# Making the first pair's gates of layer 1's second mixture in parts during the causal attention

## The chip, the cores and the metric

The kernel runs on one core of one Trainium2 chip. A core has five engines with a queue each: PE (matrix products, whose results go into one of the kernel's eight "bank" tiles of 128 x 512), DVE (vector work), ACT (functions of one operand), POOL (general work) and SP, which here only issues transfers. Between engines, semaphores carry the dependences. The metric is device time in microseconds (us), smaller is better. Before the change it is 1533.77 us, the median of 3 runs (1532.04 to 1535.4).

## The reference

A stack of four layers on x of 4 images (b) x 512 tokens x 128 features, fp32. Each layer is half a mixture of experts, an attention (or a scan), and half a mixture again. Cut to what the change touches, layer 1's attention and the mixture that follows it:

```python
x = x + _L1_attn_ref(_layernorm(x), Wq1, Wk1, Wq2, Wk2, Wv, Wo, bo)
#   logits = A1 * A2 * SCALE per head (16 heads), causal, softmax, times v, times Wo
x = x + 0.5 * _L1_ffn_ref(_layernorm(x), gate_weight, w_gate, w_up, w_down, ws_gate, ws_up, ws_down)

def _L1_ffn_ref(...):
    scores = jax.nn.sigmoid(x @ gate_weight.T)            # 8 experts
    topk_w, topk_idx = jax.lax.top_k(scores, 2)
    topk_w = 2.5 * topk_w / (topk_w.sum(-1, keepdims=True) + 1e-20)
    combine = einsum('tk,tke->te', topk_w, one_hot(topk_idx))
    y_e = (silu(x @ w_gate[e].T) * (x @ w_up[e].T)) @ w_down[e].T
    return einsum('te,teh->th', combine, y) + shared      # shared: one more expert, no gate
```

After it come layer 2's mixture, scan and mixture, and then layer 3's first mixture.

## The kernel before, in words

x stays in SBUF as one tile for each image, xs[b], 128 tokens by 4 by 128. Layer 1 uses all experts on all tokens: two experts of 64 rows fill the 128 partitions, so there are 4 chunks and a fifth for the shared expert.

The attention (`attention`, called by `l1_attn`) goes through 16 units, an image and four of its 16 heads each, and each unit through 4 key blocks j. Its order on PE, DVE, ACT and POOL is written out by hand: the scores of the next unit (L610, then the largest on DVE, L627 and L631, and the exponentials on ACT, L644, or a subtraction on POOL, L642), the transposed weights of this one (L655, L664, L666), and their products with the values (L677, into acc, copied by ACT at L761). Between them, small generators get a turn: `begin_next` the next image's norm and factors, and `go_on` whatever `after(b)` returned when image b was through (`ended`, L789 and L1236). In layer 1 `after` is None. Each key block offers up to two such turns. Rows q_a and k_a are fetched by SP for units ahead (L1206) and multiplied at L1213.

The mixture (`l1_ffn`) works on a pair of images. `normed_T` makes the norm of both (statistics L160 and L161 on DVE; variance to the power -1/2 and offsets on POOL, L164 to L169; application by turns on DVE, L178, and ACT, L174), transposes them on PE (L187) and copies them to nT (L1049). `scored` makes the scores (L1058), a sigmoid follows (L1083), then the choice of two experts, some 17 small instructions on DVE (L218 to L231 twice, L1108 to L1115), giving comb. `to_rows` transposes comb (L1071), copies it (L1073) and stores it to DRAM as rows, expert by token (L1075); the transfer at L1124 reads the rows back, each spread over 64 partitions, as cb, 2 transfers of 512 KB for each image. For each chunk `up` makes two products (L1092, L1093), a sigmoid (L1096) and two multiplications on DVE (L1097, L1098); POOL multiplies the gated chunks by cb (L1147); `down` is the second product (L1135), and L1153 adds it to xs[b].

The stage after the attention ("chain") is a generator `behind` for each pair: this mixture, layer 2's mixture, scan and mixture, and the tokens of layer 3's mixture. `skewed(gens, lag)` gives each live generator one step a round, the second from round `lag` on. POOL's order there is the order of this program; PE, DVE, ACT and SP are ordered by the planner, from its own estimates. It may also place work of this stage earlier, where its inputs are there and its memory is not taken from the stage's own pool; norms and nT come from a pool that lives through the whole kernel (`work`).

The tiles of the stage's own pool (decay, gates, cb, h and others) take memory that the attention used.

Of the kernel before, what the change touches and what calls it, by code (L numbers as in the profile page):

```python
# [9 lines left out]
FP = mybir.dt.float32  # L10
# [31 lines left out]
def kernel(ctx: ExitStack, tc: tile.TileContext, a: dict, out: bass.AP):  # L42
# [95 lines left out]
    def load_T(ap, rows, cols, name, tag=None):  # L138

        dst = pools["w"].tile([cols, rows], FP, name=name, tag=tag or name)  # L140
        m = min(rows, P)
        k = rows // m
        raw = stage.tile([m, k, cols], FP, name=f"raw_{name}", tag="raw")
        nc.sync.dma_start(raw, ap.rearrange("(k m) c -> m k c", m=m))
        ps = bank(f"ps_{name}")
        for i in range(k):
            nc.tensor.transpose(ps[:cols, i * m : (i + 1) * m], raw[:, i, :], ident[:m, :m])
        copy(dst, ps[:cols, :rows])
        return dst


# [914 lines left out]

    def to_rows(pool, gates, i, tag):

        pc = bank(f"gT_{tag}")
        for t in range(NT):  # L1070
            nc.tensor.transpose(pc[:E, t * P : (t + 1) * P], gates[:, i * NT + t, :], ident)  # L1071
        gT = pool.tile([E, S], FP, name=f"gT_{tag}", tag="gT")
        nc.scalar.copy(gT, pc[:E, :])  # L1073
# [3 lines left out]

    def l1_ffn(pool, i, bs):
        tag = f"f1{i}_{bs[0]}"
        G = len(bs) * NT  # L1080
        nTs = yield from normed_T(pool, bs, tag)
        sc = pool.tile([P, G, E], FP, name=f"sc_{tag}", tag="sc1")
        nc.scalar.activation(sc, scored(nTs, l1["gate"], tag), AF.Sigmoid)  # L1083
        order = [NC] + list(range(NC))
# [16 lines left out]

        up(0, 0)
        yield
        m1, s1 = route(pool, sc, G, "0")
        rest = without(pool, sc, m1, G, -4.0, "0")
        m2, s2 = route(pool, rest, G, "1")
        total = pool.tile([P, G], FP, name=f"total_{tag}", tag="total")
        nc.vector.tensor_tensor(total, s1, s2, ALU.add)  # L1108
        nc.vector.tensor_scalar(total, total, 1e-20, None, ALU.add)
        nc.vector.reciprocal(total, total)  # L1110

        comb = pool.tile([P, G, E], FP, name=f"comb_{tag}", tag="comb")
        nc.vector.tensor_tensor(comb, m1, m2, ALU.add)
        nc.vector.scalar_tensor_tensor(comb, comb, 2.5, sc, ALU.mult, ALU.mult)
        nc.vector.tensor_tensor(comb, comb, bc(total, [P, G, E]), ALU.mult)  # L1115
        up(0, 1)
        yield
        cbs = []
        for x, b in enumerate(bs):
            rows = to_rows(pool, comb, x, f"{b}_{tag}")  # L1120

            cb = pool.tile([P, NC, S], FP, name=f"cb{b}_{tag}", tag="spread", bufs=4)
            for u in range(2):
                nc.sync.dma_start(  # L1124
                    cb[u * I1 : (u + 1) * I1],
                    bass.AP(tensor=rows.tensor, offset=rows.offset + u * S, ap=[[0, I1], [2 * S, NC], [1, S]]),
                )
# [90 lines left out]

    def l1_attn(beside, begun):
        begin_, fetch_, project_, future, early = begun  # L1220
        with tc.tile_pool(name="attn1", bufs=2) as pool:
# [13 lines left out]
            def residual(b, po):  # L1235
                nc.vector.tensor_tensor(xs[b], po, xs[b], ALU.add)  # L1236

            attention(pool, "a1_", begin, project, residual, l1["wo"], lambda h: future, None,
                beside(pool), fetch,
# [224 lines left out]
    def whole(parts):  # L1464
        for _ in parts:
            pass
# [57 lines left out]
    with tc.tile_pool(name="weights12", bufs=1) as mid:  # L1524
# [12 lines left out]
        with tc.tile_pool(name="ahead1", bufs=2) as ahead:  # L1537
# [15 lines left out]

            l1_attn(lambda pool: prep_l3_ffn(xs[0]), begun)

        def behind(pool, bs):
            yield from l1_ffn(pool, 1, bs)
            yield from l2_ffn(pool, 0, bs)
# [10 lines left out]
        with tc.tile_pool(name="chain", bufs=2) as pool:  # L1569
# [13 lines left out]
            with tc.manual_schedule(engines={mybir.EngineType.Pool}):  # L1583
                whole(skewed([behind(pool, bs) for bs in pairs], 8))
        pools["w"] = wpool
# [54 lines left out]
```

## Time and profile before

| what | us |
|---|---|
| median of 3 runs | 1533.77 |
| the profiled execution | 1513.06 |
| its span, first to last instruction | 1511.3 |
| attention of layer 1, from the first scores to proj_a | 515.76 to 740.15 |
| chain stage, from there to the last indirect transfer's issue | 740.15 to 1012.1 |
| PE busy, of the span | 1271.2 (84%) |
| DVE, ACT, POOL busy | 880.3, 682.8, 694.0 |

The profile is of one execution. A group line of it reads: line of the kernel, engine, operation, written tile <- read tiles, shapes, count, then busy time; a timeline line gives start and length, and in brackets how long the engine stood idle before it and what ended that. PE's clock is given as a share of full speed. Where a line belongs to a helper (norms, transposes), the tile's name tells which call it is: names ending in _f are of a mixture, in _a of an attention.

### The profile page before, as it was taken

What the parts mean: (1) busy time and instruction counts of PE and PEld (TensorE: products, weight loads), DVE (VectorE), ACT (ScalarE), POOL (GpSimd) and SP (SyncE); (2) the same over time, 40 slices, a digit from 0 to 9 for tenths busy, and PEclk for the clock granted to TensorE, in tenths of its full rate; (3) what the DMA queues carried; (4) which work ended last, traced back from release to release, by engine and by line L of the source; (5) the groups of instructions that cost most, each with busy time, mean ns of one, the idle gap of its engine ahead of it and who ended that gap; (6) DMA issues with size and microseconds to landing.
All of it is one profiled execution on the core that took longest, in us unless ns stands there. A gap on an engine that the chain in (4) does not pass through costs nothing.

```text
span 1511.3 us, 28774 instructions
## 1 busy us (share of the span) xinstructions
PE 1271.2 (84%) x10645; PEld 816.7 (54%) x10645; DVE 880.3 (58%) x2890; ACT 682.8 (45%) x1431; POOL 694.0 (46%) x808
## 2 busy tenths in 40 slices
PE   4787999995969999999878878729689999998394
PEld 3465666774746666667555656616433333333173
DVE  5236767763355657767456566525367787774343
ACT  1235877871422367767522222103236655564042
POOL 5346767871433678868323111464431223312343
PEclk9897999995999999999999888759879999999597
DMA  9410240002513884231022000023105000000223
GB/s 262 101 53 22 79 170 12 9 7 73 151 37 65 223 258 145 87 121 44 4 64 49 1 1 1 28 71 91 60 15 177 15 7 10 14 3 15 78 78 112
DMA packets 100660, 106.21 MB, mean 70 GB/s; under 512 B 9084, under 2 KB 73832, under 8 KB 100520
## 3 DMA queue, kind: packets, MB, share of 16 engines
q1 hardware_dynamic: 91752, 90.11, 20.7%
q0 software_dynamic: 6656, 13.22, 2.5%
q8 instruction: 84, 1.38, 0.4%
q10 hardware_dynamic: 2112, 1.05, 0.3%
q14 instruction: 56, 0.46, 0.1%
HBM read 62.49 MB, written 41.85 MB: 69 GB/s over the span
## 4 chain that ended last, share of the span: by engine, by line
PE 70%; DVE 9%; POOL 8%; DMA 5%; issue 5%; ACT 3%; SPq 1%; POOLq 0%; ACTq 0%; DVEq 0%
PE s_a L610 13%; PE t_a L655 10%; PE o_f L515 6%; PE h_f L479 6%; PE acc_a L677 5%; PE acc_a L749 5%; PE y_f L1329 3%; PE t_a L610 3%; POOL disp_f L408 2%; PE ot_a L768 2%; PE gu_f L1092 2%; PE lg_f L322 1%; POOL rstd_f L165 1%; DVE low L699 1%; PE gu_f L1093 1%
## 5 line engine op out<-in xcount | busy, mean ns | idle before, releaser
L642 POOL TENSOR_SCALAR sc_a<-sc_a,top_a 128x128 f32<-128x128 f32 (+3 forms) x256 | 274.8, 1089 | 84.7 <-DVE top_a L627 55.8
L610 PE MATMUL s_a<-k_a,q_a 32*128 32x512 f32 (+3 forms) x1536 | 263.4, 544 | 7.0 <-DVE top_a L631 3.7
L719 ACT ACTIVATE w_a<-t_a 128x512 f32<-128x512 f32 x256 | 140.4, 595 | 116.6 <-PE t_a L610 86.9
L699 DVE TENSOR_REDUCE low<-s_a 128x1 f32<-128x512 f32 x256 | 163.4, 684 | 45.4 <-PE t_a L610 32.7
L655 PE MATMUL t_a<-ident,sc_a 128*128 128x128 f32 x1280 | 174.3, 283 | 4.3 <-DVE top_a L631 3.8
L610 PE MATMUL t_a<-ql_a,k_a 32*128 32x512 f32 x512 | 167.2, 644 | 0.3 <-DVE low L699 0.2
L501 POOL DMA_INDIRECT res_f<-y_f,back_f x112 | 109.8, 980 | 124.6 <-ACT y_f L500 90.3
L655 PEld LDWEIGHTS t_a<-ident,sc_a 128*128 128x128 f32 x1280 | 144.6, 144 | 41.0 <-issue 16.5
L644 ACT ACTIVATE sc_a<-sc_a,top_a 128x128 f32<-128x128 f32 (+3 forms) x256 | 135.0, 575 | 12.8 <-DVE top_a L631 12.2
L610 PEld LDWEIGHTS s_a<-k_a,q_a 32*128 32x128 f32 x1536 | 91.5, 187 | 79.1 <-issue 41.9
L664 ACT ACTIVATE w_a<-t_a 128x256 f32<-128x256 f32 (+2 forms) x192 | 94.2, 526 | 71.0 <-PE t_a L655 70.8
L408 POOL DMA_INDIRECT disp_f<-n_f,to_f x96 | 94.8, 988 | 56.2 <-issue 35.8
L515 PE MATMUL o_f<-w_l,h_f 128*128 128x128 f32 (+1 forms) x896 | 109.6, 277 | 0.0
L515 PEld LDWEIGHTS o_f<-w_l,h_f 128*128 128x128 f32 (+1 forms) x896 | 102.1, 184 | 8.0 <-DVE back_f L464 4.4
L479 PE MATMUL h_f<-dT_f,w_l 128*128 128x320 f32 (+1 forms) x256 | 104.1, 544 | 2.8 <-ACT dT_f L457 2.8
L677 PE MATMUL acc_a<-w_a,vpad 128*32 128x128 f32 x2560 | 98.2, 280 | 0.0
L666 ACT COPY w_a<-t_a 128x256 f32<-128x256 f32 (+2 forms) x192 | 93.5, 527 | 5.0 <-PE t_a L655 4.7
L631 DVE CUSTOM_DVE_ANT_0 sc_a<-s_a,future 128x128 f32<-128x128 f32 (+3 forms) x128 | 62.3, 487 | 47.7 <-PE s_a L610 39.0
L1147 POOL TENSOR_TENSOR h_f<-h_f,cb_f 128x512 f32<-128x512 f32 x32 | 40.7, 1286 | 104.4 <-DVE h_f L1098 62.7
L631 DVE CUSTOM_DVE_ANT_0 sc_a<-s_a,table 128x128 f32<-128x128 f32 (+3 forms) x128 | 62.3, 487 | 43.5 <-PE s_a L610 38.3
L500 ACT ACTIVATE y_f<-o_f,d_f 128x128 f32<-128x128 f32 (+1 forms) x112 | 39.0, 394 | 98.0 <-DVE o_f L495 94.1
L749 PE MATMUL acc_a<-w_a,vpad 128*32 128x256 f32 x1024 | 82.1, 391 | 1.0 <-DVE low L699 0.9
(341 smaller groups left out, 2182.8 us busy)
## 6 DMA issues: line engine op xcount, KB each, us to landing
fac_a<-fac_a_sb SPq DMA_DIRECT2D x36, 256.0 KB, 4.9
disp_f<-zeros_f SPq DMA_DIRECT2D x4, 2080.0 KB, 10.6
d_f<-disp_f SPq DMA_DIRECT2D x32, 260.0 KB, 3.0
w_l<-in_L_ffn_w_dram SPq DMA_DIRECT2D x16, 512.0 KB, 7.2
cb_f<-rows_f SPq DMA_DIRECT2D x16, 512.0 KB, 8.4
q_a<-fac_a SPq DMA_DIRECT2D x32, 256.0 KB, 3.5
k_a<-fac_a SPq DMA_DIRECT2D x32, 256.0 KB, 3.8
r_f<-res_f SPq DMA_DIRECT2D x16, 256.0 KB, 2.8
```

The lines of the kernel that those rows point to most:

```text
L408: nc.gpsimd.indirect_dma_start(out=self.to[c][i0 + t][:, :], out_offset=bass.IndirectOffsetOnAxis(ap=to[:, c, t : t + 1], axis=0), in_=ns[ ...
L479: nc.tensor.matmul(ps[u][:, :cap], w1[:, e, (c + u) * P : (c + u + 1) * P], dT, start=True, stop=True)
L515: nc.tensor.matmul(po[:m, s, :], h[:, c, s * P : s * P + m], w2[:, e, c, :], start=(c == 0), stop=(c == NC - 1),)
L610: nc.tensor.matmul(ps[:, n0:n1], q[r : r + SLOT, i * P : (i + 1) * P], k[r : r + SLOT, n0:n1], start=True, stop=True)
L631: nc.vector.tensor_tensor_reduce(sc, banks[r][:, :n], more, -1.0, HUGE, ALU.add, ALU.min, top)
L642: nc.gpsimd.tensor_scalar(sc, sc, top, None, ALU.subtract)
L644: nc.scalar.activation(sc, sc, AF.Exp, bias=top, scale=-1.0)
L655: nc.tensor.transpose(ps[:, x * n + j * P : x * n + (j + 1) * P], st["sc", u, i, r0 + x][:, j * P : (j + 1) * P], ident,)
L677: nc.tensor.matmul(st["acc", u][r * SLOT : (r + 1) * SLOT, i * P : (i + 1) * P], vpads[b % 2][:, j, g * 4 + r, :], st["w", u, i, r][:, j * ...
L699: nc.vector.tensor_reduce(st["low", u][:, i, c : c + 1], ps, AX.X, ALU.max, negate=True)
L719: nc.scalar.activation(w, ps, AF.Exp)
L749: nc.tensor.matmul(acc[r * SLOT : (r + 1) * SLOT, n0:n1], vpads[b % 2][:, j, g * 4 + r, :], st["w", u, j, r][:, n0:n1], start=(j == 0 and ...
```

## The change

Five edits. `l1_ffn` for the first pair no longer makes its norm, transposes, scores, choice and rows; a new generator `l1_early` makes them in 20 parts, handed to the attention as `after(1)`, so that its turns run from the end of image 1 on (`after` of the other images is empty). Its norm is the fine form: two tiles of statistics or of application a part. Since ACT computes exponentials in the attention, the sigmoid is made there as 1 / (1 + exp(-s)), by an exponential on ACT and an addition and a reciprocal on DVE. The choice is taken out into `chosen`, which the second pair uses as before, all at once. Small tiles of `l1_early` come from a new pool ("gates10") opened around the attention, its rows' copies from `work`. The lag of the chain stage goes from 8 rounds to 4. `norms`, `route`, `without`, `transposed` and `scored` are called as they are.

```diff
@@ -147,6 +147,14 @@
             nc.tensor.transpose(ps[:cols, i * m : (i + 1) * m], raw[:, i, :], ident[:m, :m])
         copy(dst, ps[:cols, :rows])
         return dst
+
+    def made_of(parts):
+
+        while True:
+            try:
+                next(parts)
+            except StopIteration as end:
+                return end.value
 
 
     def norms(srcs, dsts, tag, on="vector", fine=False):
@@ -1064,23 +1072,74 @@
             )
         return plg[:, : len(nTs) * NT * E].rearrange("p (g e) -> p g e", e=E)
 
-    def to_rows(pool, gates, i, tag):
+    def chosen(pool, sc, G, tag):
+
+        m1, s1 = route(pool, sc, G, "0")
+        yield
+        rest = without(pool, sc, m1, G, -4.0, "0")
+        m2, s2 = route(pool, rest, G, "1")
+        yield
+        total = pool.tile([P, G], FP, name=f"total_{tag}", tag="total")
+        nc.vector.tensor_tensor(total, s1, s2, ALU.add)
+        nc.vector.tensor_scalar(total, total, 1e-20, None, ALU.add)
+        nc.vector.reciprocal(total, total)
+        comb = pool.tile([P, G, E], FP, name=f"comb_{tag}", tag="comb")
+        nc.vector.tensor_tensor(comb, m1, m2, ALU.add)
+        nc.vector.scalar_tensor_tensor(comb, comb, 2.5, sc, ALU.mult, ALU.mult)
+        nc.vector.tensor_tensor(comb, comb, bc(total, [P, G, E]), ALU.mult)
+        return comb
+
+    def l1_early(pool, bs, got):
+
+
+        tag = f"f11_{bs[0]}"
+        G = len(bs) * NT
+        ns = [work.tile([P, NT, D], FP, name=f"n{b}_{tag}", tag="n", bufs=3) for b in bs]
+        yield from norms([xs[b] for b in bs], ns, tag, "both", True)
+        nTs = []
+        for n, b in zip(ns, bs):
+            yield
+            nT = work.tile([P, S], FP, name=f"nT{b}_{tag}", tag="nT", bufs=4)
+            copy(nT, transposed(n, f"{b}_{tag}"))
+            nTs.append(nT)
+            yield
+        sc = pool.tile([P, G, E], FP, name=f"sc_{tag}", tag="sc1")
+        for x in range(len(bs)):
+            yield
+
+            nc.scalar.activation(
+                sc[:, x * NT : (x + 1) * NT], scored(nTs[x : x + 1], l1["gate"], f"{x}_{tag}"), AF.Exp, scale=-1.0
+            )
+        yield
+        nc.vector.tensor_scalar(sc, sc, 1.0, None, ALU.add)
+        nc.vector.reciprocal(sc, sc)
+        comb = yield from chosen(pool, sc, G, tag)
+        rows = []
+        for x, b in enumerate(bs):
+            yield
+            rows.append(to_rows(work, comb, x, f"{b}_{tag}", "n", 3))
+        got[:] = nTs, rows
+
+    def to_rows(pool, gates, i, tag, of="gT", bufs=2):
 
         pc = bank(f"gT_{tag}")
         for t in range(NT):
             nc.tensor.transpose(pc[:E, t * P : (t + 1) * P], gates[:, i * NT + t, :], ident)
-        gT = pool.tile([E, S], FP, name=f"gT_{tag}", tag="gT")
+        gT = pool.tile([E, S], FP, name=f"gT_{tag}", tag=of, bufs=bufs)
         nc.scalar.copy(gT, pc[:E, :])
         rows = dram.tile([E, S], FP, name=f"rows_{tag}", tag=f"rows_{tag}")
         nc.sync.dma_start(rows, gT)
         return rows
 
-    def l1_ffn(pool, i, bs):
+    def l1_ffn(pool, i, bs, early=None):
         tag = f"f1{i}_{bs[0]}"
         G = len(bs) * NT
-        nTs = yield from normed_T(pool, bs, tag)
-        sc = pool.tile([P, G, E], FP, name=f"sc_{tag}", tag="sc1")
-        nc.scalar.activation(sc, scored(nTs, l1["gate"], tag), AF.Sigmoid)
+        if early:
+            nTs, rows = early
+        else:
+            nTs = yield from normed_T(pool, bs, tag)
+            sc = pool.tile([P, G, E], FP, name=f"sc_{tag}", tag="sc1")
+            nc.scalar.activation(sc, scored(nTs, l1["gate"], tag), AF.Sigmoid)
         order = [NC] + list(range(NC))
         hs = {}
 
@@ -1099,31 +1158,23 @@
             hs[x, k] = h
 
 
-        up(0, 0)
-        yield
-        m1, s1 = route(pool, sc, G, "0")
-        rest = without(pool, sc, m1, G, -4.0, "0")
-        m2, s2 = route(pool, rest, G, "1")
-        total = pool.tile([P, G], FP, name=f"total_{tag}", tag="total")
-        nc.vector.tensor_tensor(total, s1, s2, ALU.add)
-        nc.vector.tensor_scalar(total, total, 1e-20, None, ALU.add)
-        nc.vector.reciprocal(total, total)
-
-        comb = pool.tile([P, G, E], FP, name=f"comb_{tag}", tag="comb")
-        nc.vector.tensor_tensor(comb, m1, m2, ALU.add)
-        nc.vector.scalar_tensor_tensor(comb, comb, 2.5, sc, ALU.mult, ALU.mult)
-        nc.vector.tensor_tensor(comb, comb, bc(total, [P, G, E]), ALU.mult)
-        up(0, 1)
-        yield
+        if not early:
+            up(0, 0)
+            yield
+            comb = made_of(chosen(pool, sc, G, tag))
+            up(0, 1)
+            yield
+            rows = []
         cbs = []
         for x, b in enumerate(bs):
-            rows = to_rows(pool, comb, x, f"{b}_{tag}")
+            if not early:
+                rows.append(to_rows(pool, comb, x, f"{b}_{tag}"))
 
             cb = pool.tile([P, NC, S], FP, name=f"cb{b}_{tag}", tag="spread", bufs=4)
             for u in range(2):
                 nc.sync.dma_start(
                     cb[u * I1 : (u + 1) * I1],
-                    bass.AP(tensor=rows.tensor, offset=rows.offset + u * S, ap=[[0, I1], [2 * S, NC], [1, S]]),
+                    bass.AP(tensor=rows[x].tensor, offset=rows[x].offset + u * S, ap=[[0, I1], [2 * S, NC], [1, S]]),
                 )
             cbs.append(cb)
         for x, b in enumerate(bs):
@@ -1216,7 +1267,7 @@
 
         return begin, fetch, project, future, {}
 
-    def l1_attn(beside, begun):
+    def l1_attn(beside, begun, after):
         begin_, fetch_, project_, future, early = begun
         with tc.tile_pool(name="attn1", bufs=2) as pool:
             def begin(b):
@@ -1235,7 +1286,7 @@
             def residual(b, po):
                 nc.vector.tensor_tensor(xs[b], po, xs[b], ALU.add)
 
-            attention(pool, "a1_", begin, project, residual, l1["wo"], lambda h: future, None,
+            attention(pool, "a1_", begin, project, residual, l1["wo"], lambda h: future, after,
                 beside(pool), fetch,
             )
 
@@ -1551,10 +1602,15 @@
             with tc.tile_pool(name="ffn10", bufs=2) as pool:
                 whole(skewed([followed(pool, bs) for bs in pairs], 12))
 
-            l1_attn(lambda pool: prep_l3_ffn(xs[0]), begun)
+            early = []
+            with tc.tile_pool(name="gates10", bufs=1) as pool:
+                l1_attn(
+                    lambda _: prep_l3_ffn(xs[0]), begun,
+                    lambda b: l1_early(pool, pairs[0], early) if b == 1 else iter(()),
+                )
 
         def behind(pool, bs):
-            yield from l1_ffn(pool, 1, bs)
+            yield from l1_ffn(pool, 1, bs, early if bs[0] == 0 else None)
             yield from l2_ffn(pool, 0, bs)
             yield from l2_attn(pool, bs)
             yield from l2_ffn(pool, 1, bs)
@@ -1581,7 +1637,7 @@
                 nc.vector.tensor_copy(row, flag.to_broadcast([P, P]))
                 l2["row"].append(row)
             with tc.manual_schedule(engines={mybir.EngineType.Pool}):
-                whole(skewed([behind(pool, bs) for bs in pairs], 8))
+                whole(skewed([behind(pool, bs) for bs in pairs], 4))
         pools["w"] = wpool
     prep_l3_attn()
     with tc.tile_pool(name="padded", bufs=1) as pool:
```

## The prediction

> **What bounds the kernel now.** I began with the page: PE is busy 84% of the span and the chain that ended last runs through PE for 70%. So a stage full of PE work gets longer by any PE work put into it, and a stage where PE waits gets shorter when the wait goes. The two stages of this change are one of each kind. I took them from the chain of waits and the timeline.
>
> The first is the start of the stage after the causal attention, about 740 us. The chain of waits there (start, length, what):
>
> ```profile
> 740.62 0.59 ACT nT_f L1049
> ...
> 746.76 4.41 issue
> 751.17 0.71 PE gT_f L1071 x4
> ...
> 752.55 1.46 DMA rows_f<-gT_f
> ...
> 754.67 6.85 DMA cb_f<-rows_f
> ...
> 761.68 3.71 POOL h_f L1147 x3
> ...
> 765.82 1.67 POOL rstd_f L165
> ...
> 791.43 6.77 DMA cb_f<-rows_f
> ```
>
> The last product of the attention (proj_a L789) ends at 740.15. From there until 761.58 the end waits for the first pair's gates: transposes, scores, the choice on DVE (the 4.41 us in which PE does nothing), rows out to DRAM, rows spread back in. Then come three multiplications on POOL, and only then the second pair's norm. POOL's timeline shows why the pairs are tied:
>
> ```profile
> 740.35 0.52 POOL L1571 MEMSET decay<- 128x512 f32 x1 [9.27 <-PE proj_a L789]
> 740.81 1.84 POOL L1574 MEMSET gates<- 128x1024 f32 x2
> 761.68 3.71 POOL L1147 TENSOR_TENSOR h_f<-h_f,cb_f 128x512 f32<-128x512 f32 x3 [19.03 <-DMA cb_f<-rows_f]
> 765.48 0.25 POOL L164 TENSOR_SCALAR rs_f<-mv_f 128x8 f32<-128x8 f32 x1
> ```
>
> POOL's order is written by hand here: pair 2's rs_f at 765.48 stands behind the multiplications, which waited 19.03 us for cb_f. The first line also says from when anything of this stage can start: a memset reads nothing, yet it waited for proj_a, so the stage's memory is handed over only when the attention is through.
>
> The second stage is the attention itself, in windows of one unit each (an image and four heads; cut at the copies L761; columns: window, length, busy time of PE, PEld, DVE, ACT, POOL with counts, granted clock, DMA share, GB/s):
>
> ```profile
> 598.87:611.70 12.83, 12.65 (x169) 9.19 (x169) 9.85 (x45) 9.73 (x23) 9.71 (x10) 1.00 0.36 115
> ...
> 659.59:665.63 6.04, 6.04 (x25) 4.63 (x25) 2.46 (x10) 4.42 (x10) 3.00 (x3) 0.50 0.00 0
> 651.27:670.50 19.23, 16.55 (x169) 11.74 (x169) 11.12 (x49) 11.47 (x27) 12.18 (x14) 0.82 0.23 74
> 670.50:681.75 11.25, 11.25 (x159) 8.03 (x158) 8.09 (x36) 9.39 (x23) 9.75 (x10) 1.00 0.31 97
> ```
>
> An undisturbed unit takes 11.25 us and is all PE; one in which an image ends takes 12.83; but the one at 651.27, of that same kind, takes 19.23. The difference is the norm of the first pair, which the planner has already drawn into the attention, in one lump. The timelines of ACT and PE there:
>
> ```profile
> 658.29 0.88 ACT L174 ACTIVATE n_f<-x,off_f,rstd_f 128x128 f32<-128x128 f32 x2 [4.15 <-POOL off_f L169]
> 659.59 1.65 PE L610 MATMUL s_a<-k_a,q_a 32*128 32x384 f32 x4 [2.50 <-ACT w_a L664]
> ```
>
> ACT stood 4.15 us before n_f, its exponentials came late, PE stood 2.50 us, and then ran at clock 0.50 for 6.04 us (the window at 659.59).
>
> **What the Trainium skill says.** "TensorE: Matmul & The Clock Gate", What's actually happening: PE falls to half clock after an idle window of about 3.4 us and needs as long in work to recover. The trace agrees in kind: half clock for 6.04 us, after a pause of only 2.50. "Perfetto Trace Analysis", Tensor Engine Instruction: ACT, DVE and GpSimd are strictly first in, first out. That is the 4.15 us above. "ScalarE: Activation LUTs", What ACT_TABLE_LOAD costs: a change of function set costs about 1.28 us, and a drain. The load before the first sigmoid takes 1.28 us at 743.42; with the exponential in the attention it stays a single one.
>
> **The change, part by part.**
>
> *Removed at 740 us.* Before, the spread of the rows is issued at 754.02. Now rows are in DRAM by about 690, and the spread has only to wait until the stage's memory is free: proj_a, 740.15. The SP queue holds nothing else then (its last entry before is at 690.97), so I take 740.3. From issue to first use it took 761.58 - 754.02 = 7.56 us; cb_f is there at 747.9, which is 13.7 us sooner. Are the factors h_f there? PE makes one every 1.72 us (L1092 0.86 and L1093 0.86), the first from 740.2; with the table load, ACT 0.60 and two DVE products of 0.69, the second, which is the first to need cb_f, is ready by 746 and the fifth by 751.3. POOL at 1.26 us each from 747.9 wants the fifth at 751.7. So they are in time, by 0.4 us at the tightest.
>
> *The lag of 4 for 8.* Pair 1 loses five rounds (norm two, transposes one, the two around the choice), so its first four multiplications now lie in rounds 1 to 4, and pair 2's first POOL work is in round 4 behind the fourth, where it was behind the third: 1.3 us given back. rs_f: 747.9 + 4 x 1.26 = 752.9 against 765.48, 12.6 us sooner.
>
> *From there to pair 2's own gates.* rs_f to cb_f was 765.48 to 798.3, 32.8 us: POOL pow 1.67, transposes, scores, the choice threaded between products on DVE, rows, spread. The same instructions stay. PE was busy 46 of the 58.1 us from 740.15 to 798.25; without pair 1's transposes, scores and gate transposes (1.0 + 1.9 + 1.6 at the clock it had) 41.5 must fit into 45.5. It fits, but tightly: I give no further gain here. Then, in POOL's order, pair 1's second norm stands behind two multiplications of pair 2 and no longer behind four, and before pair 2's third: about 0.4 us net. Stage: -13 us. Bounds: -20, if every wait shrinks to what PE has to do (58 - 41.5 = 16.5, and some 3 more if the clock, 0.90 there, stays full), and -5, if pair 2, one round further behind pair 1 from here on, waits for pair 1's POOL work in later rounds.
>
> *Added in the attention.* It begins after image 1 ends (about 653 us) with two parts per key block: 20 parts, 2.5 units, done near 690; the attention lasts until 740. PE: 8 transposes (1.04), 8 score products (0.9, half of the 1.85 that 16 take), 8 gate transposes (1.04): 3.0 us, nothing to hide them, as PE has no idle time there. DVE: 17 instructions of the choice at 0.22 = 3.7, add and reciprocal 0.4, one copy 0.69: 4.8 us in three units that have 3.1 us idle each. ACT: one copy, two small exponentials, two row copies: 0.6 + 0.4 + 1.1 = 2.1, against 1.9 idle a unit. SP: two row transfers, which could stand before the last fetches of q and k; the last is issued at 690.97 and used at 706.24 (k_a, L1213), so about 10 us late is free. PE, in order, may also wait for comb before the gate transposes, a DVE part of 1.3 us behind four reductions: I take 1.5 us for such waits, between 0 and 6.
>
> *Recovered in the attention.* The lump becomes eight parts: two tiles of statistics at a time, and the application one part (about 1.4 us of PE work) after POOL's rs, rstd, off. Image 3's norm, which is already in such parts, lies in 634.68 to 651.27, where PE was busy 17.1 of 18 us from 634 to 652: no long pause. The lump cost 19.23 - 12.83 = 6.4 us. It is 2.5 us from mv to off, and ACT now waits at most about half of its 4.15 us; PE should not fall to half clock. I take 6.4 back, between 0 and 6.4. Attention: 3.0 + 1.5 - 6.4 = -2.
>
> Sum: -13 - 2 = -15 us on the profiled span of 1511.3. That execution took 1513.06 in all and the timed median is 1533.77, 1.5% more than the span, so -15.2 there: **1518.5 us**.
>
> **Rivals.** *More than that* (1507 to 1512): PE never waits between 740 and 798, -20, with the attention at -2 to -5. Against it: POOL's order still makes pair 1 wait for pair 2's gates. *Half of it comes back* (1524 to 1530, worked at 1527): the planner orders PE, DVE and ACT anew and pair 2 runs a round later beside pair 1. For it: near 970 to 982 POOL is filled with pair 1's 16 indirect transfers at 1.26 us each and pair 2's norms stand between them; two more ahead cost 2.5 us. -5 in the chain and -2 give -7. *Nothing measurable*: the attention pays 6.4 + 3 + 2 of the 13, with the lump's stall still there. *Slower*: new pauses of PE in the attention. The place is units 9 to 11, PE's in-order waits for nT and comb and the banks they hold; the price is that of the pause seen, 6.4 us each with the half clock after it. If the first is not recovered, the sum is -13 + 3 + 6.4n: from the second new pause (n = 2 gives +2.8) the change loses, with three it is +9.2, 1543 us. Against it: after each transposition the parts leave at least one part before the result is used.
>
> **How the numbers follow.** My own forecast 0.62, its own range 1513.5 to 1523.5; more 0.10; half 0.16; nothing 0.05; slower 0.07. Differences under 0.2%, 3.1 us, can't be told from none. Faster 0.88, same 0.05, slower 0.07. For 8 in 10 the range takes most of the two neighbours: 1509 to 1529.
>
> **What would show it.** Right: cb_f issued at the end of the attention, without rows_f ahead of it; POOL's 19 us wait down to about 5; pair 2's rs_f 13 us after proj_a rather than 25; the unit with the norm at 13 to 15 us at clock 1.00, the two after it at about 12.5. Wrong: a clock of 0.5 in any of these units; the attention longer than before; pair 2's cb_f less than 10 us sooner after proj_a; or the distance from pair 2's cb_f to the last indirect transfer (210 us now, 798 to 1008) grown by over 3 us.

## The result, and the profile after

The changed kernel takes 1515.24 us (median of 4 runs, 1511.73 to 1520.24) where the kernel before, run beside it, takes 1532.9 (4 runs, 1529.47 to 1535.4): a ratio of 0.9895, with an interval from 0.9868 to 0.9921, so about 16 us less. The prediction was 1518.5 us, within 1509 to 1529. The sum is nearly right. The two numbers it was made of are not: the attention, put at -2 us, got longer, and the stage after it, put at -13, lost about 20.

All stages below are cut as in the table of before: the attention from the first scores to proj_a, the chain stage from there to the start of the last indirect transfer's issue (1011.14 in before; the 1012.1 of the table of before is where that issue ends). One thing has to be known to read them. The runs came from several chips, and the kernel before took medians of 1530.27, 1532.41 and 1514.13 us on three of them. Every ratio is to runs on the same chip. The profile of before that the prediction used (1513.06 us) is as short as the runs on the third, so a second profile of before, from the first chip (1535.56 us), stands beside it.

| us | before, first profile | before, again | after |
|---|---|---|---|
| span | 1511.3 | 1533.8 | 1514.3 |
| attention | 224.39 | 223.0 | 229.61 |
| chain stage | 271.0 | 274.4 | 252.2 |
| pair 1's spread cb_f issued, from proj_a's end | 13.87 | 14.19 | 0.13 |
| pair 2's rs_f, from proj_a's end | 25.3 | 26.1 | 13.8 |
| pair 1's second rs_f, from proj_a's end | 64.0 | 63.4 | 44.9 |

Against the second profile the two stages give +6.6 - 22.2 = -15.6 us, which is the measured 16; against the first, +5.2 - 18.8 = -13.6. The other stages of the two profiles of before differ by about 20 us in places that no edit touches (layer 1's first mixture and layer 3 above all), so spans are not compared.

The start of the chain stage, in the chain of waits of after (start, length, what):

```profile
749.50 0.86 PE gu_f L1151 x2
...
757.07 0.70 DVE h_f L1156
757.82 1.28 POOL h_f L1198
...
761.97 1.27 POOL h_f L1198
763.33 0.26 POOL rs_f L172
763.66 1.67 POOL rstd_f L173
...
784.31 7.33 DMA cb_f<-rows_f
```

The wait for the rows is gone from it: from proj_a's end at 749.50 the chain runs through PE's products, the factors on DVE and four multiplications on POOL to pair 2's norm, and the only spread left in it is pair 2's own. The timeline of SP shows the two halves of the first pair's rows apart:

```profile
693.56 2.82 SPq L1131 DMA_DIRECT2D rows_f<-gT_f  x2
...
749.63 2.57 SPq L1175 DMA_DIRECT2D cb_f<-rows_f  x4
```

The rows go out 56 us before they are read back, the spread is issued 0.13 us after proj_a. POOL's timeline, to be held against the four lines of before (there 19.03 us of waiting for cb_f):

```profile
749.70 0.53 POOL L1627 MEMSET decay<- 128x512 f32 x1 [9.27 <-PE proj_a L797]
...
757.82 3.73 POOL L1198 TENSOR_TENSOR h_f<-h_f,cb_f 128x512 f32<-128x512 f32 x3 [5.67 <-DVE h_f L1156]
761.97 1.27 POOL L1198 TENSOR_TENSOR h_f<-h_f,cb_f 128x512 f32<-128x512 f32 x1 [0.42 <-DVE h_f L1157]
763.33 0.25 POOL L172 TENSOR_SCALAR rs_f<-mv_f 128x8 f32<-128x8 f32 x1
...
785.12 1.26 POOL L1198 TENSOR_TENSOR h_f<-h_f,cb_f 128x512 f32<-128x512 f32 x1 [1.44 <-DVE h_f L1157]
791.77 2.50 POOL L1198 TENSOR_TENSOR h_f<-h_f,cb_f 128x512 f32<-128x512 f32 x2 [5.38 <-DMA cb_f<-rows_f]
794.36 0.24 POOL L172 TENSOR_SCALAR rs_f<-mv_f 128x8 f32<-128x8 f32 x1
```

POOL now waits 5.67 us, for factors. Count the multiplications ahead of 791.77, where POOL waits for pair 2's cb_f: 3, 1, and four more between 772 and 786 (the last is shown), all eight of pair 1. In before POOL came to that wait with seven done:

```profile
792.33 1.28 POOL L1147 TENSOR_TENSOR h_f<-h_f,cb_f 128x512 f32<-128x512 f32 x1 [4.38 <-DVE h_f L1098]
798.34 4.96 POOL L1147 TENSOR_TENSOR h_f<-h_f,cb_f 128x512 f32<-128x512 f32 x4 [4.73 <-DMA cb_f<-rows_f]
804.14 0.24 POOL L164 TENSOR_SCALAR rs_f<-mv_f 128x8 f32<-128x8 f32 x1 [0.83 <-DVE mv_f L161]
```

The line at 798.34 holds four: pair 1's eighth stands there behind multiplications of pair 2, and pair 1's second norm (804.14) needs what the eighth gives. This order turns out to be worth more than half of the change.

The attention, in windows of a unit (window, length, busy time of PE, PEld, DVE, ACT, POOL, granted clock, DMA share, GB/s):

```profile
655.12:669.24 14.12, 13.64 (x174) 9.83 (x175) 12.16 (x56) 10.27 (x24) 11.14 (x14) 1.00 0.41 131
669.24:682.28 13.04, 13.04 (x165) 9.76 (x164) 8.73 (x38) 10.84 (x27) 11.43 (x11) 1.00 0.26 81
682.28:702.41 20.13, 15.23 (x181) 10.27 (x181) 13.30 (x55) 11.18 (x25) 9.72 (x9) 0.92 0.16 49
702.41:713.68 11.27, 11.09 (x155) 7.80 (x153) 8.15 (x36) 9.24 (x22) 9.82 (x10) 1.00 0.05 14
```

The unit with the norm went from 19.23 to 14.12 us, at full clock. The one after it pays 1.8 us over an undisturbed 11.25 and all of that is PE work. The third pays 8.9, and PE is busy for only 15.23 of it. The timelines of PE and DVE there:

```profile
692.01 0.91 PE L1127 MATMUL gT_f<-ident,comb_f 128*8 128x128 f32 x4 [4.90 <-DVE comb_f L1089]
```

```profile
683.90 1.61 DVE L1264 TENSOR_TENSOR q_a<-q_a,q_a 128x512 f32<-128x512 f32 x1
685.44 0.18 DVE L1114 TENSOR_SCALAR sc_f<-sc_f 128x64 f32<-128x64 f32 x1
...
688.82 0.23 DVE L234 TENSOR_TENSOR mask<-eq,first 128x64 f32<-128x64 f32 x1
688.96 0.42 DVE L639 CUSTOM_DVE_ANT_0 sc_a<-s_a,future 128x256 f32<-128x256 f32 x1
...
691.64 0.22 DVE L1089 TENSOR_TENSOR comb_f<-comb_f,total_f 128x64 f32<-128x64 f32 x1
```

PE stands 4.90 us in front of the gate transposes, for comb. DVE had been busy without a break since 683.90: a product of q_a, then thirteen small instructions in a row (685.44 to 688.96: the addition and the reciprocal of the sigmoid, then eleven of the choice), then the four reductions of the scores that wait behind them, then comb. In the windows of PE the clock is 0.55 from 692.00 to 695.80. So one pause of the rival's kind did come, in one of the units it named.

### The profile page after: what moved, and what is told of

The parts are those of the page before. It is cut to its first block, busy times and chain, and to the rows that moved or that the text cites. A ratio compares the mean times of both kernels' runs of the same rounds, so it can differ in the third digit from the quotient of the medians.

```text
span 1514.3 us, 28772 instructions
## 1 busy us (share of the span) xinstructions
PE 1278.2 (84%) x10645; PEld 817.5 (54%) x10645; DVE 881.6 (58%) x2893; ACT 682.6 (45%) x1431; POOL 696.5 (46%) x808
## 3 DMA queue, kind: packets, MB, share of 16 engines
q8 instruction: 84, 1.38, 0.4%
q10 hardware_dynamic: 2112, 1.05, 0.3%
## 4 chain that ended last, share of the span: by engine, by line
PE 66%; DVE 9%; POOL 8%; issue 7%; DMA 6%; ACT 2%; SPq 1%; POOLq 0%; ACTq 0%; DVEq 0%
PE s_a L618 13%; PE t_a L663 8%; PE h_f L487 5%; PE acc_a L757 5%; PE o_f L523 5%; PE acc_a L685 5%; PE y_f L1380 4%; PE t_a L618 3%; PE ot_a L776 2%; POOL disp_f L416 2%; POOL res_f L509 2%; PE gate_f L1397 2%; PE lg_f L330 1%; PE T_f L195 1%; DVE low L707 1%
## 5 line engine op out<-in xcount | busy, mean ns | idle before, releaser
L650 POOL TENSOR_SCALAR sc_a<-sc_a,top_a 128x128 f32<-128x128 f32 (+3 forms) x256 | 276.5, 1096 | 84.4 <-DVE top_a L635 58.5
L663 PE MATMUL t_a<-ident,sc_a 128*128 128x128 f32 x1280 | 170.9, 279 | 6.1 <-DVE top_a L639 5.3
L663 PEld LDWEIGHTS t_a<-ident,sc_a 128*128 128x128 f32 x1280 | 142.1, 142 | 41.2 <-issue 15.6
L172 POOL TENSOR_SCALAR rs_f<-mv_f 128x4 f32<-128x4 f32 (+1 forms) x23 | 5.3, 232 | 194.8 <-DVE mv_f L169 194.3
```

What stands on the lines that cost most here:

```text
L650: nc.gpsimd.tensor_scalar(sc, sc, top, None, ALU.subtract)
L663: nc.tensor.transpose(ps[:, x * n + j * P : x * n + (j + 1) * P], st["sc", u, i, r0 + x][:, j * P : (j + 1) * P], ident,)
```

## The experiments

Two questions were open: is it PE's in-order wait for comb or DVE's run of small instructions that costs the third unit, and why did the chain stage lose so much more than 13 us? The lag is the number of rounds that pair 2 runs behind pair 1.

**The kernel before, again** (unchanged, one run, as a second profile of before):

> The kernel before, a second profile. If the first profile of before (1513.06 us) was an unusually short execution, this one takes about 1530 us and the extra lies in stages that the change doesn't touch (the attention of layer 3 above all); from the end of layer 1's attention to the last indirect transfer it is again 271 us, within 3. If the change itself lengthens layer 3's attention by 10 us (as the two first profiles would have it), this one takes 1513 us again, with that attention as in the first.

It took 1535.56 us; its stages are in the table above. They bear out the shape of before (units of 17.8 us with the norm, 11.2 after it; 19.64 us of POOL waiting for cb_f) and show how much stages differ between executions: the attention began at 525.9 us for 515.76. The chain stage's 274.4 us are just outside the 3 us that I allowed, and of the 22.5 us between the two spans layer 3's attention has only 6.

**Room between comb and the transposes.** Four empty parts ahead of `to_rows`, so that PE reaches the gate transposes later:

```diff
         comb = yield from chosen(pool, sc, G, tag)
         rows = []
+        for _ in range(4):
+            yield
```

> Four empty parts between the choice and the gates' transposes. Theory: PE's 4.90 us wait for comb and the half clock after it are what makes the unit from 682 us 20.1 us long instead of 11.3; without the wait it is 12.5 to 13.5, the attention 6 to 8 us shorter, and the time 0.990 to 0.9935 of after, some 0.984 of before. Rival: the wait only moves to the banks (DVE's lump of 13 small instructions holds up the scores' reductions in any case); then the unit stays above 17 us and the time is that of after (0.9895).

Measured: 1514.32 us, ratio 0.9902 [0.9877, 0.9928], no different from after. The wait for comb is gone, and PE's pause has moved to the scores, whose banks DVE had not emptied (timeline of PE, then the window, of this run):

```profile
689.41 1.41 PE L618 MATMUL s_a<-k_a,q_a 32*128 32x384 f32 x2 [1.09 <-DVE top_a L639]
```

```profile
689.41:695.20 5.79, 5.79 (x22) 4.42 (x22) 4.66 (x22) 2.77 (x5) 4.07 (x4) 0.52 0.02 3
```

After a pause of only 1.09 us PE runs at half clock over the 5.79 us of this window. The third unit took 18.3 us and the fourth 12.3, together 30.6 for 31.4: the place of the wait is not the cause.

**The choice in thin parts.** `chosen` is written out in parts of two or three DVE instructions, each followed by an empty part (the core of it; total and comb are parted in the same way):

```diff
-        comb = yield from chosen(pool, sc, G, tag)
+        comb = yield from chosen_thin(pool, sc, G, tag)
...
+            nc.vector.tensor_reduce(mx, src, AX.X, ALU.max)
...
+            nc.vector.tensor_tensor(eq, src, bc(mx, [P, G, E]), ALU.is_equal)
+            nc.vector.tensor_tensor(eq, eq, bc_mid(e_rank, [P, G, E]), ALU.mult)
+            yield
+            yield
...
+            nc.vector.tensor_reduce(first, eq, AX.X, ALU.max)
...
+            nc.vector.tensor_tensor(mask, eq, bc(first, [P, G, E]), ALU.is_equal)
```

> The early choice cut into six parts of two or three DVE instructions, each followed by an empty part. Theory: what lengthens the unit from 682 us from 11.3 to about 20 us is DVE, which works off 13 small instructions and a q_a product (5.1 us) before it comes to the next scores, so that PE stands and falls to half clock; in parts of 0.7 us no such pause arises, no window at half clock lies in units 9 to 13, each unit is at 11.3 to 12.5 (13.5 where an image ends), the attention takes 222 to 224 us instead of 229.7, and the time is 0.985 to 0.987 of before. Rival, that PE's own added work (3 us) and not the lump is the loss: attention above 227 us, time 0.989 to 0.990.

Measured: 1512.9 us, ratio 0.9867 [0.9845, 0.9889]. The attention takes 225.05 us for 229.61, its units from the ninth on are 14.1, 13.0, 13.2, 12.8, 14.6 and 11.2, and the clock stays full (windows of this run, around the end of the choice):

```profile
683.20:696.40 13.20, 12.65 (x172) 9.05 (x172) 10.37 (x42) 9.78 (x23) 9.76 (x10) 1.00 0.23 70
696.40:709.20 12.80, 11.95 (x158) 8.45 (x156) 11.16 (x47) 9.47 (x22) 9.92 (x10) 1.00 0.07 19
```

The same instructions, in smaller parts, and the 4.9 us and the half clock are gone, though the q_a product of 1.60 us is there again (685.10). So the run of small instructions on DVE is needed for that loss. The attention stays a microsecond over the 222 to 224 that I wrote, and its units are at 12.8 to 13.2 where I wrote 11.3 to 12.5, so something of the rival is true as well. In the time of the whole kernel the step from 0.9895 is within the intervals; it is the traces that show it.

**The sigmoid by ACT's own function.** In `l1_early`, Sigmoid for the exponential, without the addition and the reciprocal:

```diff
-                sc[:, x * NT : (x + 1) * NT], scored(nTs[x : x + 1], l1["gate"], f"{x}_{tag}"), AF.Exp, scale=-1.0
+                sc[:, x * NT : (x + 1) * NT], scored(nTs[x : x + 1], l1["gate"], f"{x}_{tag}"), AF.Sigmoid
...
-        nc.vector.tensor_scalar(sc, sc, 1.0, None, ALU.add)
-        nc.vector.reciprocal(sc, sc)
```

> The changed kernel with the sigmoid by ACT's own function in the early gates, without the addition and the reciprocal on DVE. ACT changes its function set there and back, twice if exponentials stand between the two images' scores: 2 to 4 loads of 1.28 us each, in front of exponentials that PE waits for. Theory (the exponential form is what keeps the attention whole): the units with the scores and the choice get 2 to 8 us longer, attention 231 to 238 us for 229.6, the stage after it as before at 252 to 254; ratio 0.990 to 0.995. Rival (ACT has the time, and DVE's 13 instructions in a row are what hurts, now two fewer): attention 227 to 230 us, ratio 0.987 to 0.990.

Measured: 1494.3 us (on the third chip, where before takes 1514.13), ratio 0.9878 [0.9853, 0.9904], so the rival's figures. The attention takes 228.16 us. The four loads are there (timeline of ACT):

```profile
673.21 1.28 ACT L1110 ACT_TABLE_LOAD   x1
674.51 0.20 ACT L1110 ACTIVATE sc_f<-lg_f 128x32 f32<-128x32 f32 x1
674.77 1.28 ACT L672 ACT_TABLE_LOAD   x1
...
678.43 1.28 ACT L1110 ACT_TABLE_LOAD   x1
679.73 0.20 ACT L1110 ACTIVATE sc_f<-lg_f 128x32 f32<-128x32 f32 x1
679.94 1.28 ACT L672 ACT_TABLE_LOAD   x1
```

With them the second unit takes 14.3 us for 13.0, and the third is 16.7 for 20.1, with two of the thirteen instructions gone. That the exponential keeps the attention whole, which I had taken for granted, is not borne out: either form is as good here, and the intervals overlap.

**The coarse norm in the early gates** (one run):

```diff
-        yield from norms([xs[b] for b in bs], ns, tag, "both", True)
+        yield from norms([xs[b] for b in bs], ns, tag, "both", False)
```

> The change with the early norm in its coarse form (all statistics in one part, all applications in the next). Theory: ACT again stands about 4 us before n_f, PE pauses over 2 us and falls to half clock: the unit from 655 us takes 17.5 to 19.5 us where after has 14.1. Rival, that the lump was costly only because the planner put it at a bad place: 14 to 15.5 us.

Measured: 1523.42 us, attention 231.85. Here ACT waits 5.32 us for off_f (1.97 in after); the units are 21.6 and 16.8 for 14.1 and 13.0, while the third falls to 11.5, as the choice now lies in the second. The first is even longer than I wrote, with 10.2 us at half clock, so the fine form is what recovers the lump. The second unit shows something more (timeline of PE, then a window, of this run):

```profile
692.48 1.13 PE L663 MATMUL t_a<-ident,sc_a 128*128 128x128 f32 x8 [1.38 <-DVE top_a L639]
695.51 0.60 PE L1127 MATMUL gT_f<-ident,comb_f 128*8 128x128 f32 x4 [1.12 <-DVE comb_f L1089]
```

```profile
690.00:700.00 10.00, 7.50 (x107) 5.20 (x105) 8.17 (x33) 6.00 (x12) 3.61 (x3) 1.00 0.12 36
```

The thirteen instructions stand in a row here too (DVE, 688.34 to 691.95), but no slow q_a product stands ahead of them (that unit's took 0.93 us). PE pauses 1.38 and 1.12 us for 4.90, and the clock stays full. So the run alone cost 2.5 us of pauses here, the slow q_a alone 0.55 in the thin form, and the two together 4.90 and the half clock; each is read from one trace, in units that differ in other work too.

**One part at a time.** The early gates with the old lag (8 for 4 in the changed kernel), and the lag alone (4 for 8 in the kernel before):

```diff
-                whole(skewed([behind(pool, bs) for bs in pairs], 4))
+                whole(skewed([behind(pool, bs) for bs in pairs], 8))
```

> The change, with the lag of the last stage back at 8. Theory: pair 2's norm then stands in POOL's order behind pair 1's later multiplications, about 10 us later than with 4; the early gates of pair 1 alone gain little: 0.995 to 1.000 of before. Rival, that the early gates bring the gain and the lag only keeps step: 0.988 to 0.992.

> The kernel before, with nothing changed but the lag, 4 for 8. Theory: the early gates are needed; pair 2's norm now stands before pair 1's multiplications in POOL's order and can be made during pair 1's wait, but both pairs' choices compete for DVE and PE, pair 1's cb_f comes as late as before, and pair 1's later POOL work comes behind pair 2's: 0.996 to 1.002 of before. Rival, that the order on POOL is the whole story: pair 2's cb_f lands some 20 us sooner (775 to 780 us) and the time is 0.986 to 0.991 of before.

Measured: 1.0017 [1.0003, 1.0032] for the early gates alone, 0.9964 [0.9951, 0.9977] for the lag alone. The first is just above what its theory gave, the second within it, and neither rival came. The two don't add up to 0.9895: -0.36% and +0.17% apart, -1.05% together. With the early gates and a lag of 8, pair 2's norm stands behind six multiplications (rs_f at 22.8 us after proj_a), and POOL later waits 14.87 us for its cb_f: the stage takes 270.3 us. With a lag of 4 and the old rows, pair 2's norm comes first of all (rs_f at 2.8), but pair 1's second norm is as late as before (62.2), and the stage takes 266.8.

**One round less.** The changed kernel with a lag of 3 and, on the same chip, the thin form with 2:

```diff
-                whole(skewed([behind(pool, bs) for bs in pairs], 4))
+                whole(skewed([behind(pool, bs) for bs in pairs], 3))
```

> The change with lag 3: pair 2's rs_f stands behind three multiplications, as in the kernel before. Theory: rs_f 1.3 to 3 us sooner after proj_a (11 to 12.5 for 13.8), but the product that waits for the fourth multiplication now stands before pair 2's transposes on PE again, rs_f to cb_f grows from 28 to over 30 us; time within 0.2% of after (0.9875 to 0.9915 of before). Rival, one place in the queue is worth its 1.3 to 3 us to the end: 0.9870 or less.

> As before it, with the lag at 2. Theory that PE, busy 39.7 of the 42.2 us from the end of the attention to pair 2's cb_f, bounds that stretch with lag 4: pair 2's rs_f comes 2.5 to 3 us sooner, its cb_f at most 3 us sooner, and the time changes by less than 0.2% against the one with lag 4. Rival, that pair 2's latency is still what counts: cb_f 4 to 8 us sooner and a time 0.3 to 0.5% lower.

Measured: 0.9959 [0.9939, 0.9979] for 3, so one round costs 0.64%, where I had counted on no difference; and 0.9895 [0.987, 0.9919] for the thin form with 2, against 0.9867 with 4, where the intervals overlap. With 3 the stage takes 260.8 us for 252.2 (252.9 in the thin form, on the chip of this run). POOL's timeline has the pattern of before again, three multiplications ahead of the norm and pair 1's eighth behind the wait:

```profile
760.77 0.25 POOL L172 TENSOR_SCALAR rs_f<-mv_f 128x8 f32<-128x8 f32 x1
...
764.33 1.30 POOL L1198 TENSOR_TENSOR h_f<-h_f,cb_f 128x512 f32<-128x512 f32 x1 [0.86 <-DVE h_f L1157]
...
793.42 4.96 POOL L1198 TENSOR_TENSOR h_f<-h_f,cb_f 128x512 f32<-128x512 f32 x4 [4.85 <-DMA cb_f<-rows_f]
799.20 0.24 POOL L172 TENSOR_SCALAR rs_f<-mv_f 128x8 f32<-128x8 f32 x1 [0.81 <-DVE mv_f L169]
```

And PE's timeline shows a second cost of that order (first this run, then after):

```profile
765.68 1.31 PE L1186 MATMUL o_f<-wd1T,h_f 128*128 128x128 f32 x8 [3.60 <-POOL h_f L1198]
766.80 1.91 PE L195 MATMUL T_f<-ident,n_f 128*128 128x128 f32 x8
```

```profile
763.29 1.16 PE L1186 MATMUL o_f<-wd1T,h_f 128*128 128x128 f32 x8 [0.34 <-POOL h_f L1198]
...
766.00 0.27 PE L195 MATMUL T_f<-ident,n_f 128*128 128x128 f32 x1
```

PE is in order, and the product of the fourth multiplication stands ahead of pair 2's transposes T_f. With the fourth behind the norm on POOL, PE waits 3.60 us for it, and T_f starts 6.0 us after rs_f (5.9 in before). With the fourth ahead of the norm, in after, that wait is 0.34 us, and T_f starts 2.7 us after rs_f (763.33 to 766.00). With a lag of 2 pair 2's times are as its theory has them (rs_f 2.7 us sooner than with 4, the use of cb_f 0.7; T_f 2.4 us after rs_f), but the median is 0.28% higher and not the same: only six multiplications of pair 1 stand ahead of that cb_f, and pair 1's second norm comes at 52.5 us for 44.0.

**The same round in the kernel before.** This is the test of that reading: pair 1 has five rounds more in the kernel before, so a lag of 9 makes the same POOL order there as 4 does in the changed kernel. Nothing else is changed.

```diff
-                whole(skewed([behind(pool, bs) for bs in pairs], 8))
+                whole(skewed([behind(pool, bs) for bs in pairs], 9))
```

> The kernel before with a lag of 9 rounds, nothing else changed. Pair 1 has five rounds more there than in the changed kernel, so a lag of 9 puts POOL's work in the same order as the changed kernel's lag of 4: pair 2's first norm behind four multiplications of pair 1, and pair 1's last multiplication ahead of pair 2's first. Theory (POOL's order, one round, is worth several us of the stage): pair 2's rs_f about 1.3 us later than in the kernel before (26 to 27 us after proj_a), pair 1's second rs_f no longer behind pair 2's cb_f, at 45 to 56 us instead of 64; stage after the attention 4 to 10 us shorter than the 271 to 274 us of the kernel before; ratio 0.993 to 0.998. Rival (the order matters only together with the early gates, or the 8.6 us between lags 3 and 4 was the planner's other work): pair 1's second rs_f at 60 us or later, stage within 3 us, ratio 0.998 to 1.003.

Measured: 1506.25 us, ratio 0.9946 [0.9923, 0.997]; the stage takes 258.2 us, and pair 2's rs_f is at 26.8. Pair 1's second rs_f, at 58.9, is less early than I wrote, though on the theory's side of the rival's 60, and the stage lost more than I wrote, 12.8 us against the first profile of before. Part of that is perhaps the chip's, on which the stage of the changed kernel, with ACT's sigmoid, is 6.6 us shorter than in after; and the execution profiled, 1501.28 us, is 5 us under the median. POOL's timeline has four multiplications ahead of the norm and two lines at the wait in place of the four:

```profile
761.11 4.95 POOL L1147 TENSOR_TENSOR h_f<-h_f,cb_f 128x512 f32<-128x512 f32 x4 [19.28 <-DMA cb_f<-rows_f]
766.15 0.25 POOL L164 TENSOR_SCALAR rs_f<-mv_f 128x8 f32<-128x8 f32 x1
...
795.67 2.50 POOL L1147 TENSOR_TENSOR h_f<-h_f,cb_f 128x512 f32<-128x512 f32 x2 [5.16 <-DMA cb_f<-rows_f]
798.26 0.24 POOL L164 TENSOR_SCALAR rs_f<-mv_f 128x8 f32<-128x8 f32 x1
```

T_f starts 2.4 us after rs_f here, for 5.9 in before. With the wait for the first cb_f as long as ever, one number gives 0.54%. The crossing from one order to the other is worth about as much in both kernels: 8.2 us here (0.54% of 1514.13), 9.8 us from lag 3 to 4 in the changed one (0.64% of 1532.41). A lag moves all of pair 2's work by a round, also what the planner orders; the two waits named here are what I traced of it.

**One round more**, in the thin form (5 for 4):

> The kernel with the choice cut into thin parts, with a lag of 5 rounds for 4. Pair 2's first norm then stands behind the fifth multiplication of pair 1 too, which waits for a product that PE makes about 6 us after the fourth. Theory (4 is the round at which both sides are served): pair 2's rs_f 1 to 7 us later than with 4 (15 to 21 us after proj_a), its cb_f issue later by as much, pair 1's second norm not earlier than 42 us; stage 255 to 262 us for 252.9, ratio 0.989 to 0.993 for 0.987. Rival (what counts is only that pair 1 is not held up by pair 2, so more lag goes on gaining): pair 1's second norm before 42 us, stage under 252 us, ratio 0.982 to 0.986.

Measured: 1492.32 us, ratio 0.986 [0.9831, 0.9889]. Pair 2's rs_f and pair 1's second norm stay at 13.3 and 44.1 us after proj_a; the stage takes 245.4 us, as in the run with ACT's sigmoid on the same chip (245.6, lag 4). Neither theory's figures came: no later norm, and no gain beyond what the chip gives. What both took for granted failed: POOL still has four multiplications ahead of the norm, not five, and between 4 and 5 nothing that counts changes places.

## Why the prediction was right, and where it wasn't

*The issue of the spread, -13.7 us.* Right: 13.87 before, 0.13 after. The rows went out 56 us before they were read back.

*Pair 2's rs_f, 12.6 us sooner.* Nearly: 25.3 to 13.8, 11.5 sooner. The first multiplication started 8.3 us after proj_a, where I had 7.6, since by the profile it waited for its factor (DVE's h_f at 757.07) and not for cb_f: the factor I had ready by 746, 6 us after proj_a, came at 8.3.

*From rs_f to cb_f, "I give no further gain here"; and pair 1's second norm, "about 0.4 us net".* This is where the stage's sum fell short. From the lines shown, pair 1's second norm came 19.1 us sooner (64.0 to 44.9), and that is made of 11.5 for rs_f, 4.4 from rs_f to the use of cb_f (32.86 to 28.44) and 3.2 from there on (5.80 to 2.59). I counted 0 and 0.4 for the last two. Both belong to the one round that I had seen and priced at the 1.3 us that it delays rs_f. What it also does is put the fourth multiplication, for whose product PE waits, ahead of the norm rather than behind it, and pair 1's eighth ahead of the wait for pair 2's cb_f. The run with a lag of 3 keeps the early gates and takes this round away: rs_f to cb_f is 32.65 us there, which is the 32.8 that I said would stay, and the stage is 13.6 us shorter than that of the second profile of before (274.4 to 260.8; 10.2 against the first), which is about my 13. So the term was right for the gates alone, and the term of POOL's order was 0.4 us where the runs show 8.6 in the stage (260.8 to 252.2). Of these 8.6, 5.2 are there at pair 1's second norm (50.1 to 44.9); the other 3.4 arise behind it, and I didn't trace them to single waits. I had also thought of the clock as the reserve of the wider bound, and it isn't needed: with the lag of 9 in the old kernel the clock is 0.90 from proj_a's end to 792.00, and rs_f to cb_f still fell to 29.5 us.

*The lump, -6.4, between 0 and 6.4.* Right in kind: 5.1 came back in the unit with the norm (19.23 to 14.12), at clock 1.00. Against the second profile of before, where that unit took 17.8, it is 3.7. ACT's wait is 1.97 us, within "at most about half" of 4.15.

*The added work, +3.0.* Right: in the thin form, where no half clock comes in between, the unit with the transposes and scores is 1.8 us longer than in before (13.0 for 11.25) and the one with the gate transposes 1.1 (14.6 for 13.5), 2.9 in all.

*The waits, +1.5 between 0 and 6.* This is the other term that was off. The second and third unit together are 10.7 us above undisturbed ones (13.04 + 20.13 - 22.50), where 4.5 were counted in all; without the added work 7.8 are left, more than the 6 that I allowed. In the thin form they are 3.4, in the two units that got nothing but parts of the choice (13.2 and 12.8 for 11.3 each). Part of these is short waits (12.65 us of PE work in a window of 13.20, 11.95 in one of 12.80); the rest I didn't split. The other 4.6 us are what the attention lost to the thirteen instructions where they stood (229.61 to 225.05; 4.1 against the run with a lag of 3, whose attention is that of after and whose chip that of the thin form). I priced the wait as "a DVE part of 1.3 us behind four reductions". The part before it is thirteen instructions long, and the planner set it behind a q_a product that took 1.61 us; together that is 5.06 us (683.90 to 688.96), in which no score is reduced.

*The signs.* Of the signs of being right all came but one, the third unit at about 12.5 us. Of the signs of being wrong two came: half clock in the third unit, and an attention longer than before. The other two did not: pair 2's cb_f is used 15.9 us sooner after proj_a (58.2 to 42.3), and from there to the last indirect transfer it is 209.9 us for 212.8. So the mechanism was right in the stage, but that the total came within 4 us is luck: the attention was 7 to 9 us worse than forecast and the stage 6 to 9 better, and the two nearly cancel.

*The rivals.* "More than that" had the chain right (-20) and the attention wrong. Its reason held too, up to pair 2's cb_f: PE is busy 39.78 of the 42.27 us from proj_a's end to there, at clock 1.00. The "slower" rival had the place right and, with one pause, about the price (7.8 us for 6.4): -13 + 3 + 6.4 n needs two to lose, and the lump, which it let stay, came back. "Half of it comes back" is what the early gates alone give with a lag of 3 (0.9959), that is, in the order of before; its own reason would make the 212.8 us above longer, and they got shorter.

## What to carry to other kernels

When a delay between two interleaved streams is changed, don't price the moved instruction alone: write out the hand-made order of the shared engine around it, and ask of each instruction that changes places what in-order engine waits for it next; one round was worth more than half of this change (0.64 of 1.05%), and by itself in the old kernel 0.54%. Work that is spread into a stage full of matrix products should come in parts no longer than what its engine can take between two of that stage's own deadlines: the same work cost 4.6 us more as thirteen instructions in a row behind a slow product than in twos and threes. The version with thin parts has the lowest ratios measured (0.9867 and, with a lag of 5, 0.986), though their intervals overlap that of after.

## What the runs showed of the hardware

PE fell to half clock after shorter pauses than I had thought it needs. The Trainium skill, "TensorE: Matmul & The Clock Gate", What's actually happening, speaks of an idle window of about 3.4 us. The runs differ from that: in the run with room between comb and the transposes, a pause of 1.09 us was followed by 5.79 us at clock 0.52, though PE was busy 2.32 of the 3.41 us from 686.27 to 689.68. The length of the pause doesn't decide it either: pauses of 1.38 and 1.12 us in the run with the coarse norm, and of up to 0.82 in the thin form, left the clock at 1.00. What does decide stays open. The half clock itself came in multiples of one length: 3.42 us in after (from 692.14), 6.83 in before (659.36), 6.82 in the run with room (689.68), 10.24 with the coarse norm (667.78).

The q_a product of 128x512 on DVE took 1.61 us at 683.90, where its shortest took 0.68. POOL's k_a product, with two operands too, ran from 683.70 for 1.28 us. The Trainium skill, "SBUF — State Buffer", SBUF: two separate sides, says that DVE and GpSimd share a pair of ports, that an operation with two SBUF inputs on DVE contends for it with one of GpSimd that reads SBUF, and that the loser waits for the whole instruction. The trace agrees here: from the end of k_a (684.98) to the end of q_a (685.51) is 0.53 us, most of a product of 0.68. The thin form shows it again, 1.60 us at 685.10, beside k_a from 684.88. It also lies on the chain of after, twice in pair 2's choice: eq L229, a product of 128x64 that took 0.23 us at 686.76, took 1.26 at 772.78 and 1.21 at 777.43, beside POOL's h_f at 772.70 and 777.30 (1.27 us each). But not all of POOL's work does this: at 670.05, in the midst of the subtractions of L650 (one tensor, 667.88 to 672.35), q_a took 0.69.

In the run with ACT's own sigmoid, each change of ACT's function set took 1.28 us and no more that the trace shows: the load starts 0.01 to 0.06 us after the activation before it (674.71 to 674.77) and the next activation 0.02 us after the load (674.49 to 674.51). The drain that the prediction names beside the 1.28 us doesn't show.
